# First top-p attention of a four-layer GNN kernel: two row tiles at a time, seven block products in place of eight

## The chip, the cores and the metric

The kernel runs on one core of a Trainium2 chip. The metric is device time in microseconds. Three runs of the kernel before have a median of 3461.52 us, from 3460.03 to 3462.5.

## What is computed

A graph of 3327 nodes with 256 features, `x`, and a dense float32 adjacency `adj` (3327 x 3327) go through four layers, each with a residual and a layernorm, `x = LN(x + layer(x))`. Layer 0 is a mean aggregation with a linear map of `[x, adj @ x / deg]`. Layer 1 is a graph convolution followed by a Mamba scan over the nodes. Layer 2 is a graph attention with a mask. Layer 3, the one that changes, is cut from the reference here:

```python
q = X @ W1.T @ W2.T
k = X @ W3.T
logits = q @ k.T / TAU
probs = jax.nn.softmax(logits, axis=-1)
idx = jnp.argsort(-probs, axis=-1)
sp = jnp.take_along_axis(probs, idx, axis=-1)
cs = jnp.cumsum(sp, axis=-1)
keep_sorted = cs - sp < TOP_P
...
A = probs * mask
return A / jnp.maximum(A.sum(-1, keepdims=True), 1e-12)
...
R = S + jnp.eye(N, dtype=X.dtype)
R = R / R.sum(-1, keepdims=True)
...
for n in range(STEPS):
    A = _top_p_attention(Xa, W1, W2, W3)
    Xf = R @ Xf
    Xa = A @ Xa
    Z = Z + Xf @ U1[n].T + Xa @ U2[n].T
h = X + Z
```

Here `S` is the adjacency, `TOP_P` is 0.9, `STEPS` is 2, and a layernorm of `h` follows. Diffusion (`R @ Xf`) and weighted sum (`A @ Xa`) are each a product of a 3327 x 3327 matrix with a 3327 x 256 matrix, once per step.

## The kernel before

The nodes lie in 26 tiles of 128 rows (`nt = 26`, padded to 3328), and 13 is `nh`. Everything is float32. The name `X` is the layer's input, held in SBUF as 26 tiles of 128 x 256. The adjacency lies in DRAM in transposed blocks (`adjT[tile]`: 128 partitions, 26 blocks of 128 columns), so that a block is at once the stationary operand of a matmul. In the names of the profile, "PE MATMUL acc<-X,at" is such a product: out, then moving and stationary operand. A product over all nodes of one row tile is 26 matmuls of 256 columns into one PSUM bank.

The work is staged in the order of the layers.

- *Layer 0* (L113 to L223). It already works on two row tiles at a time in the seven products of Strassen and Winograd. `halved` (L113) takes the two row tiles as the rows of a 2 x 2 block matrix, whose columns are the first and the second 13 nodes' tiles; the features are split in two halves of 128 (`HD`). It loads five block columns of both rows (`JS`, two DMAs on SP's queue), and VectorE makes three sums or differences of blocks, s2, s3, s4, in `cb`, and the fourth, s1, in place over the block a21. For each of the 13 block columns, seven matmuls of 128 or 129 columns follow. The sums t1 to t4 of the right side are made once. When a pair of tiles is done, VectorE (with one ScalarE copy) puts its four output blocks together from the seven results p1 to p7.
- *Layers 1 and 2.* The change leaves their order as it is. At the end of layer 2, while `X` is finished, the diffusion of tile 0 (`xf0`) is computed, and the keys `kT` and queries for the first attention too. Queries go through DRAM (`qd`).
- *First attention* (`l3p`, a loop from -1 to 25 over row tiles). `scores` (L1116) makes the 3328 logits of a row tile in four groups: two products of query and key into one two-bank PSUM tile `sc`, which has one buffer, and a ScalarE copy into `e`. `diffused` with `aggregated` (L1142, L1157) is a row of R @ X: blocks in loads of five (`J3`), 26 products, and a VectorE operation that adds the node's own part and divides by the degree. `search_short` (L1229) finds the threshold of the nucleus: 26 MAX8 operations on segments of 128 columns, six rounds of ranking the candidates (`ranked`), the exponential of the row on ScalarE, the point at which the running sum crosses (`crossing`), and one VectorE operation that sets the smaller weights of the row to zero and sums the kept ones. `attended` (L1172) is the weighted sum: four transposes of `e` through PE into a bank `tp`, a ScalarE copy into `wt`, four products with `X`, seven times over. `normalizer` gives one over the kept sum. `first` (L1376) ends a row tile: ScalarE scales the weighted sum (`xa`), PE transposes the two results and VectorE copies them to `xt` (L1386), PE multiplies with U1 and U2 of both steps, the sum so far goes to DRAM (`sd`), the products for the second step stay in SBUF as `Y` and `G`, and `key_and_query` (L879) makes key and query of the second attention.
- *Second attention* (`l3q`). It uses that the maps U1 and U2 of step two are already in `Y` and `G`: diffusion multiplies with `Y`, the weighted sum with `G`. Its order of work is written out slot by slot and pinned; its first search (lines L1366 and around) needs the score row of tile 0, and that one needs all keys of the first attention.

What sets the order. Each engine works its own instructions in one order, which is fixed when the kernel is built; engines wait for each other by semaphores. In layer 0 and the first attention a scheduler chooses that order by which instruction is ready and by priority (the score products have a raised one); pools decide how far ahead it can go, since a tile of a pool with two buffers cannot be written again until the one before the last is released. In the second attention, and wherever `keep_in_program_order` (`here`, `in_order`) stands, the order is that of the program. All loads and stores here are issued by SP, in order; one that waits for its data or buffer holds those behind it.

Of the kernel before, what the change touches and what calls it, by code (L numbers as in the profile page):

```python
# [9 lines left out]
F32 = mybir.dt.float32  # L10
BF16 = mybir.dt.bfloat16
# [31 lines left out]
DL = 1  # L43
HD = D // 2
JS = 5
KC = 416
# [3 lines left out]
def gnn_kernel(ctx: ExitStack, tc: tile.TileContext, n: int, a: dict, out: bass.AP):  # L50
# [7 lines left out]
    small = ctx.enter_context(tc.tile_pool(name="small", bufs=4))  # L58

# [53 lines left out]
    def halved(atp, cmb, psum, i, top, low, t):  # L113
# [5 lines left out]
        for j0 in range(0, nh, JS):  # L119
# [4 lines left out]
            cb = cmb.tile([P, 3, JS, P], F32, name="cb")  # L124
            a11, a12, s1, a22 = (at[:, r, h, :m, :] for r in range(2) for h in range(2))
            s2, s3, s4 = (cb[:, k, :m, :] for k in range(3))
            nc.vector.tensor_sub(s3, a11, s1)
            nc.vector.tensor_add(s1, s1, a22)
            nc.vector.tensor_sub(s2, s1, a11)
            nc.vector.tensor_sub(s4, a12, s2)  # L130
# [44 lines left out]
    with tc.tile_pool(name="l1b", bufs=1) as wpool, tc.tile_pool(name="l1at", bufs=2) as l1at:  # L175
# [3 lines left out]
        with tc.tile_pool(name="l0", bufs=1) as pool, tc.tile_pool(name="l0w", bufs=2) as work, \  # L179
# [30 lines left out]
            for i in range(nh):  # L210
                p1, p2, p3, p4, p5, p6, p7 = halved(atp, cmb, psum, i, top, low, ts)
                c = work.tile([P, 2, D + 1], F32, name="c")
                u = work.tile([P, 2, HD + 1], F32, name="u")
                nc.scalar.copy(u[:, 0, :], p1)
                nc.vector.tensor_add(c[:, 0, :HD + 1], p2, u[:, 0, :])
                u2, u3 = u[:, 0, :HD], u[:, 1, :HD]
                nc.vector.tensor_add(u2, p6, u2)
                nc.vector.tensor_add(u3, p7, u2)
                nc.vector.tensor_add(u2, p5[:, :HD], u2)
                nc.vector.tensor_add(c[:, 0, HD + 1:], p3, u2)  # L220
                nc.vector.tensor_sub(c[:, 1, :HD], u3, p4)
                nc.vector.tensor_copy(c[:, 1, HD:HD + 1], p5[:, HD:])
                nc.vector.tensor_add(c[:, 1, HD + 1:], p5[:, :HD], u3)  # L223
# [643 lines left out]
    with tc.tile_pool(name="l3", bufs=1) as pool, tc.tile_pool(name="l3d", bufs=1, space=DRAM) as dram:  # L867
# [10 lines left out]

        def key_and_query(work, ps, p, it, xt):  # L879

            h, j = divmod(it * P, half)
            for k in range(2):
                nc.tensor.matmul(ps, wkq[h][:, k, :], xt[:, k, :], start=(k == 0), stop=(k == 1))
# [205 lines left out]
        sd = dram.tile([nt, P, D], F32, name="sd")  # L1089
# [26 lines left out]
        def scores(work, psum, p, q, e):  # L1116
# [6 lines left out]
            for c0 in range(0, half, KC):  # L1123
# [3 lines left out]
                with tc.high_priority() if not p else nullcontext():  # L1127
                    for h, w in enumerate(ws):
                        k = slice(h * DA, (h + 1) * DA)
                        mm = nc.tensor.matmul(pl[:, h, :w], q[k, :], kT[p][k, c0:c0 + w], start=True, stop=True)  # L1130
                        if p:
                            here(mm)
# [7 lines left out]
                yield  # L1140

# [50 lines left out]
        def segment_tops(cand, z, m=nseg):  # L1192

            for s in range(m):
                nc.vector.max(cand[:, s * 8:(s + 1) * 8], z[:, s * SEG:(s + 1) * SEG])  # L1195
# [4 lines left out]
        def ranked(work, cand, rounds):  # L1200
# [3 lines left out]
            for r in range(rounds):  # L1204
                left = rest if r else cand
                nc.vector.max(top[:, r * 8:(r + 1) * 8], left)
                if r + 1 < rounds:
                    nc.vector.match_replace(rest, top[:, r * 8:(r + 1) * 8], left, NEG)
            return top

        def crossing(work, v, top, base, lim, add=ALU.add, reached=ALU.is_ge):
# [3 lines left out]
            nc.vector.tensor_tensor_scan(cs, ones[:, :k], top, initial=base, op0=ALU.mult, op1=add)  # L1215
            over = work.tile([P, k], F32, name="over", bufs=1)
            nc.vector.scalar_tensor_tensor(over, cs, lim, top, op0=reached, op1=ALU.mult)
            nc.vector.reduce_max(v, over, axis=AX.X)
# [5 lines left out]
        def limit(sm, total):  # L1224
            lim = t1(sm, "lim")
            nc.vector.tensor_scalar_mul(lim, total, TOP_P)
            return lim

        def search_short(work, sm, e, total, v, kept):  # L1229
# [3 lines left out]
            segment_tops(cand, e)  # L1233
            top = ranked(work, cand, RP0)
            neg = t1(sm, "neg")
            nc.vector.tensor_scalar_mul(neg, top[:, 0:1], -1.0)
            nc.scalar.activation(e, e, AF.Exp, bias=neg, accum_out=total)
# [472 lines left out]
```

## Time and profile before

| | |
|---|---|
| median of three runs | 3461.52 us |
| the profiled execution, its own time | 3468.8 us |
| its span, first to last instruction | 3466.9 us |
| mean granted TensorE clock | 0.968 |
| PE busy | 3190.3 us, 92% of the span |
| VectorE busy | 2497.6 us, 72% |
| ScalarE busy | 1742.9 us, 50% |
| loaded from HBM | 291.01 MB |

The span divides as follows. The borders are those of the first and last instruction of a kind in the timeline; busy times in us are from the view by stretches.

| stretch, us | stage | PE busy | DVE busy | ACT busy | clock | DMA share |
|---|---|---|---|---|---|---|
| 0 to 57.9 | layer 0, x and W | 47.1 | 25.7 | 12.7 | 1.00 | 0.61 |
| 57.9 to 324 | layer 0, seven products | 266.0 | 158.7 | 12.4 | 1.00 | 0.46 |
| 324 to 1354 | layer 1 | 854.2 | 878.7 | 673.5 | 0.92 | 0.35 |
| 1354 to 1700 | layer 2 | 335.3 | 245.0 | 53.6 | 0.99 | 0.44 |
| 1700 to 2605.4 | first attention | 888.7 | 419.4 | 318.1 | 1.00 | 0.19 |
| 2605.4 to 3450 | second attention | 798.4 | 768.1 | 671.9 | 0.98 | 0.21 |

How to read it. PE is TensorE's matmuls, PEld its loads of stationary operands, which overlap them; DVE is VectorE, ACT ScalarE, POOL GpSimd, SP the engine that issues the DMAs. The clock is the share of TensorE's full clock that the throttle granted. The DMA share is the mean busy share of the core's 16 DMA engines. Matmuls are pipelined, and several matmuls of one kind can stand in one line of a timeline ("x15"). A bracket at the end of a timeline's line is the idle time ahead of it and what ended it.

### The profile page before, as it was taken

How to read it: one execution, taken by the hardware profiler on the slowest of the kernel's cores; microseconds unless marked ns; L12 is line 12 of the kernel's file. 1: busy time of each engine (PE TensorE's matmuls, PEld its weight loads, DVE VectorE, ACT ScalarE, POOL GpSimd, SP SyncE). 2: the span in 40 equal slices, each digit the busy share in tenths (PEclk: the TensorE clock that was granted, in tenths of full speed). 3: DMA queues.
4: the chain of work that ended last, by engine and by line, in shares of the span. 5: the costliest groups of instructions: out<-in, count | busy, mean ns of one | idle time of the engine just before them, and what ended most of it. 6: DMA issues, size and time to landing. Idle time of an engine off the chain costs nothing. (4 is left out here: it accounts for less than half of the span.)

```text
span 3466.9 us, 45354 instructions
## 1 busy us (share of the span) xinstructions
PE 3190.3 (92%) x16429; PEld 2528.1 (73%) x16429; DVE 2497.6 (72%) x5559; ACT 1742.9 (50%) x2789; POOL 928.5 (27%) x942
## 2 busy tenths in 40 slices
PE   8999888898988766999999999999997999999996
PEld 5998757676666555888777777777775777777775
DVE  4665368999999997777535454545435999999996
ACT  1000556766767774111223333333337888888883
POOL 0000245665655653111100000000001333333333
PEclk9999989999999888999999999999999999999998
DMA  5543334444332222444211212121102122222220
GB/s 168 169 164 126 109 95 125 111 109 115 105 117 82 70 59 108 143 144 149 92 58 55 60 55 60 55 60 55 60 30 77 55 61 71 64 65 70 63 67 16
DMA packets 151760, 304.79 MB, mean 88 GB/s; under 512 B 19454, under 2 KB 65726, under 8 KB 151390
## 3 DMA queue, kind: packets, MB, share of 16 engines
q1 hardware_dynamic: 151518, 301.72, 29.1%
q8 instruction: 133, 2.18, 0.2%
q14 instruction: 109, 0.89, 0.1%
HBM read 291.01 MB, written 10.65 MB: 87 GB/s over the span
## 5 line engine op out<-in xcount | busy, mean ns | idle before, releaser
L329 POOL TENSOR_TENSOR h<-du,row 128x2048 f32<-128x2048 f32 (+1 forms) x110 | 465.6, 4233 | 346.4 <-DVE hc L329 249.8
L329 DVE TENSOR_TENSOR_SCAN h<-dA,carry,h 128x512 f32<-128x512 f32 (+1 forms) x384 | 448.8, 1221 | 18.4 <-ACT dA L336 18.3
L336 ACT ACTIVATE dA<-t,A_log 128x512 f32<-128x512 f32 (+1 forms) x448 | 292.4, 658 | 146.8 <-DVE h L329 145.2
L1183 PE MATMUL acc<-X,wt 128*128 128x256 f32 x1352 | 346.3, 393 | 11.5 <-ACT wt L1181 11.2
L1150 PE MATMUL acc<-F,at 128*128 128x256 f32 x1352 | 353.5, 387 | 1.0 <-ACT q L887 0.6
L1183 PE MATMUL acc<-G,wt 128*128 128x256 f32 x1352 | 336.6, 392 | 6.3 <-ACT wt L1114 5.9
L1183 PEld LDWEIGHTS acc<-X,wt 128*128 128x128 f32 x1352 | 244.4, 191 | 107.1 <-issue 41.3
L1054 PE MATMUL acc<-F,at 128*128 128x257 f32 x1352 | 302.1, 380 | 0.6 <-ACT r L998 0.6
L388 PE MATMUL cb<-F,at 128*128 128x256 f32 x1196 | 295.8, 396 | 6.9 <-ACT hn L408 3.4
L1183 PEld LDWEIGHTS acc<-G,wt 128*128 128x128 f32 x1352 | 250.0, 192 | 66.7 <-ACT wt L1114 36.4
L1195 DVE MAX8 cand<-e 128x8 f32<-128x128 f32 x676 | 142.2, 279 | 213.2 <-ACT e L1136 197.5
L1150 PE MATMUL acc<-X,at 128*128 128x256 f32 x1300 | 295.3, 380 | 0.0
L1150 PEld LDWEIGHTS acc<-F,at 128*128 128x128 f32 x1352 | 237.9, 190 | 75.3 <-issue 50.2
L679 PE MATMUL y<-ident,hc 128*128 128x128 f32 x1664 | 237.1, 297 | 45.6 <-DVE hc L329 45.3
L1054 PEld LDWEIGHTS acc<-F,at 128*128 128x128 f32 x1352 | 252.4, 190 | 36.0 <-issue 1.0
L679 PEld LDWEIGHTS y<-ident,hc 128*128 128x128 f32 x1664 | 211.5, 155 | 86.8 <-DVE hc L329 61.6
L388 PEld LDWEIGHTS cb<-F,at 128*128 128x128 f32 x1196 | 230.3, 199 | 57.4 <-issue 17.4
L1150 PEld LDWEIGHTS acc<-X,at 128*128 128x128 f32 x1300 | 242.3, 190 | 37.7 <-issue 6.6
L329 DVE TENSOR_TENSOR hc<-h,row 128x2048 f32<-128x2048 f32 (+2 forms) x114 | 242.9, 2133 | 11.4 <-PE y L679 4.3
L1181 ACT COPY wt<-tp 128x512 f32<-128x512 f32 (+1 forms) x182 | 93.6, 556 | 302.7 <-PE tp L1179 302.4
L1179 PE MATMUL tp<-ident,e 128*128 128x128 f32 x1352 | 195.3, 275 | 37.7 <-DVE e L1366 32.4
L1179 PEld LDWEIGHTS tp<-ident,e 128*128 128x128 f32 x1352 | 162.3, 142 | 77.9 <-issue 41.1
(383 smaller groups left out, 5761.8 us busy)
## 6 DMA issues: line engine op xcount, KB each, us to landing
at<-in_adjT SPq DMA_DIRECT2D x255, 320.0 KB, 3.0
at<-in_adjT SPq DMA_DIRECT2D x54, 832.0 KB, 4.5
row<-bc SPq DMA_DIRECT2D x80, 512.0 KB, 4.9
at<-in_adjT SPq DMA_DIRECT2D x52, 640.0 KB, 5.4
at<-in_adjT SPq DMA_DIRECT2D x52, 576.0 KB, 4.3
at<-in_adjT SPq DMA_DIRECT2D x26, 512.0 KB, 3.6
row<-bc SPq DMA_DIRECT2D x32, 384.0 KB, 4.8
at<-in_adjT SPq DMA_DIRECT2D x26, 384.0 KB, 4.0
```

The source lines that it names most:

```text
L329: return lambda *x, **k: tc.keep_in_program_order(op(*x, **k))
L336: decays.append(op(*x, **k))
L388: ten.matmul(acc, at[:, j % JC, :], X0[:, j, :], start=(j == 0), stop=(j == nt - 1))
L679: x = ten.matmul(y[:, g * P:(g + 1) * P], h[:, g, i * P:(i + 1) * P], ident, is_transpose=True, start=(first and g == 0), stop=(last and g ...
L1054: nc.tensor.matmul(acc, at[:, j, :], F[:, j0 + j, :], start=(j0 + j == 0), stop=(j0 + j == nt - 1))
L1150: nc.tensor.matmul(acc, at[:, j, :], rhs[:, j0 + j, :], start=(j0 + j == 0), stop=(j0 + j == nt - 1))
L1179: nc.tensor.transpose(pt[:, j, :], e[:, (j0 + j) * P:(j0 + j + 1) * P], ident)
L1181: copy(wt[:, :m, :], pt[:, :m, :])
L1183: nc.tensor.matmul(acc, wt[:, j, :], rhs[:, j0 + j, :], start=(j0 + j == 0), stop=(j0 + j == nt - 1))
L1195: nc.vector.max(cand[:, s * 8:(s + 1) * 8], z[:, s * SEG:(s + 1) * SEG])
```

## The change

*Layer 0.* The block sums get other signs and places: one broadcast operation makes s3 and s1 (each a sum with a21), s2 and s4 follow; the loaded blocks are no longer written over. s2 and s4 of every load are stored to a DRAM array `mixed`, one more DMA on SP's queue per load. The assembly of the outputs follows the signs and no longer uses ScalarE.

*First attention.* The loop goes over 13 pairs of row tiles. Diffusion (`diffused_pair`) and weighted sum (`attended_pair`) of a pair are made of seven products per step, 13 steps, as in layer 0 (`products`, `assembled`). The sums of X (`blocks`, t1 to t4) are made once and lie in the memory of `G`. For diffusion, a part is two steps (`JQ`): three DMAs bring a11, a12, a22 and the stored s2, s4, and one VectorE operation makes s1 and s3 from them. Tile 1, whose pair partner was done in layer 2, is diffused plainly (`diffused_first`). For the weighted sum, a step is four transposes (`turn`: two column blocks of two row tiles), a ScalarE copy into `wt`, and three VectorE operations into `sw` (`mix`). `search_short` is the same work cut into pieces: a yield after every five MAX8, after each ranking round, and the zeroing in two halves. `first` uses the PSUM tiles `tp`, and stores its part of `G` to DRAM (`gd`); two DMAs load `G` at the end of the stage.

*Order.* In this stage every PE and VectorE instruction is held to program order (`Fixed`), all of them recorded at one line. A pair is `stage` with seven diffusion steps, four score groups of one tile and one `first`; seven value steps of the weighted sum; `stage` with the other six diffusion steps, four groups and the other `first`; six value steps. `look` takes the next piece of the search at the head of a queue. Before the loop stand the scores of tile 0, the diffusion of tile 1, the scores of tile 1 and both searches.

In `unresolved`, a small product uses a `tp` tile. The load buffers `l3at` belong to the second attention alone now. The core of the diff:

```diff
@@ -121,13 +123,13 @@
             at = atp.tile([P, 2, 2, JS, P], F32, name="at")
             for r in range(2):
                 nc.sync.dma_start(at[:, r, :, :m, :], a["adjT"][2 * i + r].rearrange("p (h j) r -> p h j r", h=2)[:, :, j0:j0 + m, :])
-            cb = cmb.tile([P, 3, JS, P], F32, name="cb")
-            a11, a12, s1, a22 = (at[:, r, h, :m, :] for r in range(2) for h in range(2))
-            s2, s3, s4 = (cb[:, k, :m, :] for k in range(3))
-            nc.vector.tensor_sub(s3, a11, s1)
-            nc.vector.tensor_add(s1, s1, a22)
-            nc.vector.tensor_sub(s2, s1, a11)
-            nc.vector.tensor_sub(s4, a12, s2)
+            cb = cmb.tile([P, 4, JS, P], F32, name="cb")
+            at = at.rearrange("p r h j k -> p (r h) j k")
+            a11, a12, a21, a22, s3, s1, s2, s4 = (x[:, k, :m, :] for x in (at, cb) for k in range(4))
+            nc.vector.tensor_tensor(cb[:, :2, :m, :], at[:, ::3, :m, :], at[:, 2:3, :m, :].to_broadcast([P, 2, m, P]), op=ALU.add)
+            nc.vector.tensor_add(s2, s1, a11)
+            nc.vector.tensor_add(s4, a12, s2)
+            nc.sync.dma_start(mixed[i][:, :, j0:j0 + m, :], cb[:, 2:, :m, :])
...
+                c = work.tile([P, 2, D + 1], F32, name="c", bufs=1)
+                v, u = c[:, 0, HD + 1:], c[:, 1, HD + 1:]
+                nc.vector.tensor_copy(c[:, 0, :HD + 1], p1)
+                nc.vector.tensor_sub(v, p6, c[:, 0, :HD])
+                nc.vector.tensor_add(c[:, 0, :HD + 1], p2, c[:, 0, :HD + 1])
+                nc.vector.tensor_sub(u, v, p7)
+                nc.vector.tensor_add(v, v, p5[:, :HD])
+                nc.vector.tensor_sub(v, p3, v)
+                nc.vector.tensor_sub(c[:, 1, :HD], u, p4)
...
+        class Fixed:
+
+            def __init__(self, engine):
+                self.engine = engine
+
+            def __getattr__(self, name):
+                op = getattr(self.engine, name)
+                if not fixed:
+                    return op
+                return lambda *x, **k: tc.keep_in_program_order(op(*x, **k))
+
+        tensor, vector = Fixed(nc.tensor), Fixed(nc.vector)
...
+        def products(pa, y, w, b):
+
+            own, mix = pa[:, 0, :], pa[:, 1, :]
+            a11, a12, s1, a22, s2, s3, s4 = w
+            b11, b21, b22, t1, t2, t3, t4 = b
+            for k, (acc, x, v) in enumerate(((own[:, :HD], a11, b11), (own[:, HD:D], a12, b21), (own[:, D:D + HD], s1, t1),
+                                             (mix[:, :HD], s4, b22), (mix[:, HD:D], a22, t4),
+                                             (mix[:, D:D + HD], s2, t2), (mix[:, D + HD:], s3, t3))):
+                tensor.matmul(acc, x, v[:, y, :], start=(y == 0 and k in (0, 3)), stop=(y == nh - 1 and k in (2, 6)))
...
+        def assembled(work, pa):
+
+            p1, p2, p5, p3, p4, p6, p7 = (pa[:, k // 3, k % 3 * HD:(k % 3 + 1) * HD] if k < 6 else pa[:, 1, 3 * HD:] for k in range(7))
+            c = work.tile([P, 2, D], F32, name="c", bufs=1)
+            v, u = c[:, 0, HD:], c[:, 1, HD:]
+            vector.tensor_copy(v, p1)
+            vector.tensor_add(c[:, 0, :HD], p2, v)
+            vector.tensor_sub(v, p6, v)
+            vector.tensor_sub(u, v, p7)
+            vector.tensor_add(v, v, p5)
+            vector.tensor_sub(v, p3, v)
+            vector.tensor_sub(c[:, 1, :HD], u, p4)
+            vector.tensor_add(u, u, p5)
+            return c
...
+        def diffused_pair(quads, psum, i, b, out):
+
+            def part(j0):
+                m = min(JQ, nh - j0)
+                at = quads.tile([P, 5, JQ, P], F32, name="at", bufs=3)
+                rows = [a["adjT"][2 * i + r].rearrange("p (h j) r -> p h j r", h=2)[:, :, j0:j0 + m, :] for r in range(2)]
+                nc.sync.dma_start(at[:, :2, :m, :], rows[0])
+                nc.sync.dma_start(at[:, 2, :m, :], rows[1][:, 1])
+                nc.sync.dma_start(at[:, 3:, :m, :], mixed[i][:, :, j0:j0 + m, :])
+                cb = quads.tile([P, 2, JQ, P], F32, name="cb", bufs=2)
+                vector.tensor_tensor(cb[:, :, :m, :], at[:, 3:4, :m, :].to_broadcast([P, 2, m, P]), at[:, :3:2, :m, :], op=ALU.subtract)
+                a11, a12, a22, s2, s4, s1, s3 = (x[:, k, :m, :] for x, y in ((at, 5), (cb, 2)) for k in range(y))
+                return a11, a12, s1, a22, s2, s3, s4
...
+            pa = psum.tile([P, 2, 512], F32, name="acc")
+            ahead = part(0)
+            yield
+            for j0 in range(0, nh, JQ):
+                w, ahead = ahead, part(j0 + JQ) if j0 + JQ < nh else None
+                for j in range(min(JQ, nh - j0)):
+                    products(pa, j0 + j, [x[:, j, :] for x in w], b)
+                    yield
+            c = assembled(quads, pa)
+            for r in range(2):
+                with_own(c[:, r, :], 2 * i + r, out)
...
+        def attended_pair(quads, psum, es, b):
+
+            pa = psum.tile([P, 2, 512], F32, name="acc")
+            wts, ws = [], []
+
+            def turn(j):
+                pt = psum.tile([P, 4, P], F32, name="tp")
+                for r, e in enumerate(es):
+                    for h in range(2):
+                        tensor.transpose(pt[:, 2 * r + h, :], e[:, (h * nh + j) * P:(h * nh + j + 1) * P], ident)
+                wts.append(quads.tile([P, 4, P], F32, name="wt", bufs=4))
+                nc.scalar.copy(wts[-1], pt)
+
+            def mix():
+                wt = wts.pop(0)
+                sw = quads.tile([P, 4, P], F32, name="sw", bufs=3)
+                vector.tensor_tensor(sw[:, :2, :], wt[:, ::3, :], wt[:, 2:3, :].to_broadcast([P, 2, P]), op=ALU.add)
+                vector.tensor_add(sw[:, 2, :], sw[:, 1, :], wt[:, 0, :])
+                vector.tensor_add(sw[:, 3, :], sw[:, 2, :], wt[:, 1, :])
+                a11, a12, a21, a22, s3, s1, s2, s4 = (x[:, k, :] for x in (wt, sw) for k in range(4))
+                ws.append((a11, a12, s1, a22, s2, s3, s4))
+            for j in range(3):
+                turn(j)
+            for j in range(2):
+                mix()
+            yield None
+            for j in range(nh):
+                if j + 3 < nh:
+                    turn(j + 3)
+                if wts:
+                    mix()
+                products(pa, j, ws.pop(0), b)
+                yield None
+            yield assembled(quads, pa)
...
-            nc.vector.scalar_tensor_tensor(e, e, v, e, op0=ALU.is_ge, op1=ALU.mult, accum_out=kept)
-            yield
+            yield
+            sums = t1(sm, "sums", 2)
+            for h in range(2):
+                part = e[:, h * half:(h + 1) * half]
+                vector.scalar_tensor_tensor(part, part, v, part, op0=ALU.is_ge, op1=ALU.mult, accum_out=sums[:, h:h + 1])
+                yield
+            vector.tensor_add(kept, sums[:, :1], sums[:, 1:])
...
+            pg = psum.tile([P, 4, P], F32, name=tag).rearrange("p (k x) d -> p k (x d)", k=2)
+            for k in range(2):
+                tensor.matmul(pg[:, 0, :], xt[:, 2 + k, :], u2[:, 1, k, :], start=(k == 0), stop=(k == 1))
+            if tag == "pj":
+                nc.scalar.copy(G[:, it, :], pg[:, 0, :])
+            else:
+                g = work.tile([P, D], F32, name="s")
+                nc.scalar.copy(g, pg[:, 0, :])
+                nc.sync.dma_start(gd[it], g)
             key_and_query(work, pg[:, 1, :P], 1, it, xt[:, 2:, :])
...
+                def stage(spread, steps, groups, ends, then=lambda: None):
+                    for k in range(steps):
+                        next(spread, None)
+                        if k % 2:
+                            next(ends, None)
+                        else:
+                            next(groups, None)
+                        if k == 5:
+                            then()
+                        look()
...
+                def attend_to(i):
+                    turned[0] = attended_pair(quads, psum, (es[2 * i], es[2 * i + 1]), b)
+                    finish()
+                    next(turned[0])
...
+                for i in range(nh):
+                    ends = todo or [iter(()), iter(())]
+                    stage(spread, 7, logits(2 * i + 2), ends[0], lambda: attend_to(i))
+                    values = turned[0]
+                    if i + 1 < nh:
+                        queue.append(searches[2 * i + 2])
+                    for _ in range(7):
                         next(values)
-                        if todo is not None:
-                            next(todo)
-                        todo = first(work, psum, i, last_of(values), f, xfs[i])
-                        next(todo)
-                both(todo)
+                        look()
+                    stage(spread, 6, logits(2 * i + 3), ends[1])
+                    for _ in spread:
+                        pass
+                    finish()
+                    if i + 1 < nh:
+                        queue.append(searches[2 * i + 3])
+                    for k in range(6):
+                        if k == 3:
+                            spread = spreading(i + 2)
+                        next(values)
+                        look()
+                        if k % 3 == 2:
+                            look()
+                    c = next(values)
+                    todo = []
+                    for r in range(2):
+                        it = 2 * i + r
+                        f = normalizer(sm, kepts[0][:, it:it + 1], tots[0][:, it:it + 1])
+                        todo.append(first(quads, psum, it, c[:, r, :], f, xfs[it], "tp"))
+                        next(todo[r])
...
+            for x in (slice(0, JH), slice(JH, nt)):
+                nc.sync.dma_start(G[:, x, :], gd[x].rearrange("t p d -> p t d"))
```

## The prediction, made before the result was known

> **What bounds the kernel now.** I read the page's 40 slices first, then the busy time by stretches, then the timelines of PE and DVE inside the stage that changes, then the rows of groups for durations.
>
> ```profile
> PE   8999888898988766999999999999997999999996
> DVE  4665368999999997777535454545435999999996
> PEclk9999989999999888999999999999999999999998
> ```
> The first attention is slices 20 to 30 (1700 to 2605 us): PE full, DVE half full, clock whole. The stretches say the same, with layer 0 on top (columns after the length: busy us and count of PE, PEld, DVE, ACT, POOL; clock; DMA share; GB/s).
>
> ```profile
> 150.00:200.00 50.00, 50.00 (x450) 50.00 (x449) 30.16 (x80) 1.72 (x6) 0.00 (x0) 1.00 0.51 170
> 1900.00:1950.00 50.00, 49.52 (x247) 40.46 (x246) 22.39 (x64) 13.65 (x24) 1.95 (x3) 1.00 0.25 74
> 1950.00:2000.00 50.00, 49.76 (x249) 37.85 (x248) 22.91 (x86) 19.37 (x34) 1.12 (x3) 1.00 0.16 46
> ```
> Two markers of the DVE timeline give the period of one row tile, 1874.17 - 1839.52 = 34.65 us; it is the same for 21 tiles on end.
>
> ```profile
> 1839.52 0.68 DVE L1386 COPY xt<-pj 128x512 f32<-128x512 f32 x1
> 1874.17 0.68 DVE L1386 COPY xt<-pj 128x512 f32<-128x512 f32 x1
> ```
> The PE timeline gives prices. Fifteen matmuls of 256 columns take 3.40 us, the last one's latency 0.38 in it: (3.40 - 0.38)/14 = 0.2157 each (0.2155 over longer runs). A transpose costs 0.11. A score group (four sc matmuls) holds PE 0.9 us and about 0.2 ahead of it: 1.10.
>
> ```profile
> 1815.33 0.97 PE L1130 MATMUL sc<-kT,q 64*128 64x416 f32 x4
> 1816.23 1.56 PE L1183 MATMUL acc<-X,wt 128*128 128x256 f32 x6
> 1821.55 0.71 PE L1179 MATMUL tp<-ident,e 128*128 128x128 f32 x5
> 1822.19 0.97 PE L1130 MATMUL sc<-kT,q 64*128 64x416 f32 x4
> 1828.92 3.40 PE L1150 MATMUL acc<-X,at 128*128 128x256 f32 x15
> ```
> Per tile: 104 products x 0.2155 = 22.4, 26 transposes 2.9, four score groups 4.4, L1384 to L1398 with the key and query 4.3; 34.0, so 0.65 is gaps. PE is the bound and there is next to no wait to remove: only less PE work helps, and PE waits newly made count in full.
>
> [...] Layer 0 runs the same seven products and shows 111 (450 in 50 us); I use the trace. [...] 14.3 us idle, clock 0.50 from 2661, whole at 2676.
>
> ```profile
> 2670.78 1.54 PE L1179 MATMUL tp<-ident,e 128*128 128x128 f32 x6 [14.34 <-DVE e L1366]
> 2661.00:2664.00 3.00, 0.00 (x0) 0.00 (x0) 2.48 (x16) 2.14 (x1) 0.60 (x3) 0.50 0.00 0
> 2673.00:2676.00 3.00, 3.00 (x8) 2.10 (x7) 2.96 (x8) 2.57 (x2) 0.21 (x1) 0.50 0.00 0
> 2676.00:2679.00 3.00, 3.00 (x18) 2.02 (x18) 2.93 (x12) 1.34 (x2) 0.00 (x0) 0.96 0.00 0
> ```
> [...]
>
> **The change, part by part.** A pair is two row tiles; a step is one of its 13 rounds of seven products.
>
> *Products.* Layer 0 makes 169 steps from 59.4 to 323.9: 1.565 us each. A pair costs 13 x 1.565 = 20.35 against 104 x 0.2155 = 22.41 now: 2.06 saved. Not an eighth (2.8), since short matmuls are relatively dearer. Diffusion has 12 pairs (tile 0 belongs to layer 2, tile 1 stays plain), the weighted sum 13: 25 x 2.06 = 51.5 saved. Now the stage is 905.3 = 26 x 34.645 - 11.2 (tile 0's diffusion) + 15.7 of fill and drain. Work after: 889.6 - 51.5 = 838; per pair 65.2.
>
> *DVE work.* Per pair now 2 x (14.6 search + 1.7) = 32.6. Added: 13 mixes of wt into sw (256, 128, 128 columns, each feeding the next: 0.96 us), 12.5; seven cb differences of 512 columns at 0.65, 4.6; two assemblies of eight 128-column operations, 2.0 each; 0.4. Sum about 54 of 65: not a bound in the mean. Cover: PE's own work.
>
> *Fixed order.* It holds DVE and PE to program order, so I laid the queues of one pair side by side with the durations above. Stage 1 is seven diffusion steps, four score groups, one tile's first() (4.4) and 12 transposes: 11.0 + 4.4 + 4.4 + 1.4 = 21.2 us of PE. Then 7 value steps of 2.07, a step and its four transposes; stage 2, six diffusion steps, four groups and a first(), 18.2; 6 value steps, three of them without transposes, 10.9. Together 64.8, near the 65.2 above. Four waits come out.
> - End of stage 2: DVE does the assembly (2.0), two scalings (0.8), half a masking (2.0), then mixes 9 to 12 with 20 MAX8 (5 per 0.98) and one cb between them; mix 12 is done 13.5 after the last diffusion product, when PE has got to its third product at 12.6: 0.75.
> - DVE then still has a MAX group and three ranking rounds (0.9 each), so it is 2.9 late when PE ends the pair. Assembly, normalizer (0.35) and the ACT scaling (0.45) follow, so c is there at 2.9 + 2.0 + 0.35 + 0.45 = 5.7; PE is at its transposes after two steps, a group and two transposes, 4.45: 1.25.
> - Key and query in the same tp bank wait for ACT's copy g (0.37 plus hand-over, as 0.46 in this trace at the last tile; elsewhere other work stood between): 0.45 twice.
> - The second group of the 12 transposes waits for a tp bank that the query copy frees: 0.35.
> Sum 3.25; with one pair less affected, 11 x 3.25 + 1 = 37. Unknown from both sides: 1.0 if DVE is a tenth faster than laid out (only the bank waits stay), 6 if a tenth slower. Not below nothing: each is a new order. I take 3.25.
>
> *Queues.* Behind each waiting DVE instruction stand the MAX8 and ranking of the next tile, and PE's transposes of e wait for those; slack there is only 0.3 us. SP: 65 blocks a pair instead of 52 and one more store per tile. A part's three loads go out when PE leaves the part two before it, and SP's stores in between wait for DVE's s or ACT's g, both due earlier. Landing for 640 KB rows is 5.4 now; slack 4 to 10. Taken at nothing; 2 us a pair if the runs of 1 KB (2.5 KB now) land in 10.
>
> *Fill.* Score groups 0 and 1 stand alone: each waits for ACT to copy the one before (0.85), 2 us instead of 1.1. DVE subtracts the four blocks (7.6), then waits for tile 1's diffusion (1718.6), and does both searches one after the other: e of tile 1 is ready near 1748.7, with 32.7 us of PE work before it. That is 15.9 idle, plus 2.7 at half clock. *Drain.* With no diffusion left, PE waits for the last search (3.6), for the mixes (1.5), and does three first() without cover: 60.4 against 44.1 of work, 16.3, plus 1.5 of clock. Both 36.4, bounds 24 and 46.
>
> *G through DRAM.* The second half of G (1.7 MB) and the first at loads stand behind the last g store on SP, so the second attention's first products come about 10 us late. PE waits 14.3 us there anyway for tile 0's search (the line above), and that search's scores are now issued without products between, 2 us earlier. -2; +6 if SP takes longer.
>
> *Layer 0.* 640 KB of stores per five steps: DMA share 0.50 goes to about 0.75. The next load is ahead of the store in SP's order; combos keep their element count; the ACT copy goes. Nothing, bound +10.
>
> Sum: 838 + 37 + 36.4 = 911.4, +6; -2 and 0: +4, less 1 for waits that fall together: **+3**. The profiled execution would be 3468.8 + 3 (span 3466.9 + 3); the median of the runs shown, 3461.5, goes to **3464**.
>
> **Rivals.**
> - *Fed queues (0.24).* DVE never falls behind; waits 1.0 a pair: 838 + 12 + 30 = 880, -25 and -2: 3435. For it: DVE is half idle now. Against it: the order is rigid and its slack is tenths.
> - *DVE sets the pace (0.18).* Slower. Place: mix 12 and the half-maskings ahead of the 12 transposes. From the point where DVE ends a pair over 3 us late, each further us passes to PE. A tenth on 54 us of DVE or one late cb load makes it 6 a pair: 12 x 3 more, 3500.
> - *Layer 0's stores delay its loads (0.08).* PE is full there, so 1 us per load group shows: 39 groups, some 10 to 30 us, 3485.
> - That the seven products do not save: layer 0 shows that they do; in none of these.
>
> **Numbers.** Likeliest 0.50, own range 3452 to 3476. The range 3430 to 3496 leaves out the ends of the first two rivals, some 0.18. A measurement of this kernel can tell 0.2% (7 us) from no change: faster than 3454.6 is the first rival and a tenth of the likeliest, 0.28; slower than 3468.4 is the two slow ones and a third of it, 0.42; the rest 0.30.
>
> **What would show it.** Products: PE's 128-column matmuls at 0.111 to 0.112 each. Period of a pair 68 to 69 (69.3 now), PE idle before acc<-sw and tp<-c with DVE named, DVE 80% full. First transposes of e near 1750 and half clock after it. Second attention's start within 5 us of where it was. Wrong: a pair at 66 (first rival) or over 70 (second), or layer 0 ending after 330.

## The result, and the profile after

The changed kernel takes 3493.84 us (median of four runs, 3488.59 to 3494.34), the kernel before beside it 3462.01 us (3460.03 to 3464.72): ratio 1.0088, 95% interval 1.007 to 1.0105. It is 32 us slower; the forecast was 3464, within 3430 to 3496. The profiled execution after took 3488.6 us (span 3486.7), the one before 3468.8: only 19.8 apart, since the first lies 5 us below its kernel's median and the second 7 above its own. What the medians show beyond the 19.8 is taken up at the end of the experiments.

The page's slices for PE, VectorE and the clock, kernel after:

```profile
PE   8999888888987777999899999999978999999996
DVE  4665368999999997777577777787755999999996
PEclk9999999999999988999899999999998999999998
```
VectorE is now 7 where it was 4 to 5, and PE has a hole (7, 8) at the end of the first attention. By stretches (columns as before: busy us and count of PE, PEld, DVE, ACT, POOL; clock; DMA share; GB/s) these are layer 0, one pair in the middle of the stage, its first 56 us and its last 70:

```profile
150.00:200.00 50.00, 50.00 (x450) 50.00 (x449) 29.57 (x74) 1.19 (x4) 0.00 (x0) 1.00 0.72 249
1874.42:1942.96 68.54, 65.34 (x499) 57.03 (x498) 51.94 (x178) 24.41 (x39) 0.20 (x2) 1.00 0.25 75
1696.30:1752.70 56.40, 41.20 (x180) 28.05 (x181) 38.54 (x111) 17.68 (x20) 19.52 (x20) 0.76 0.32 97
2554.37:2624.12 69.75, 50.47 (x330) 44.09 (x330) 30.27 (x99) 15.87 (x36) 0.20 (x2) 0.93 0.13 43
```
Layer 0 still has PE full, with the DMA share at 0.72 instead of 0.51. The period of a pair is read at the same copy as before, here at every second one on VectorE's timeline:

```profile
1874.42 0.68 DVE L891 COPY xt<-tp 128x512 f32<-128x512 f32 x1
...
1942.96 0.68 DVE L891 COPY xt<-tp 128x512 f32<-128x512 f32 x1
```
A pair takes 68.54 us against 2 x 34.65 = 69.3: the products save 4.1 (the forecast's twice 2.06), and 3.3 of it are lost again, nearly all in waits. The view of PE's waits in this pair (us in total, times, longest):

```profile
PE tp L891 <- ACT c L1532: 1.4, 1, 1.4
PE tp L891 <- ACT s L1558: 0.9, 2, 0.5
PE acc L891 <- DVE sw L891: 0.6, 2, 0.5
PE tp L891 <- ACT q L903: 0.2, 1, 0.2
```
That is 3.1 us with PE idle. VectorE's longest waits in the same pair:

```profile
DVE s L891 <- PE tp L891: 8.1, 2, 4.1
DVE xt L891 <- PE tp L891: 2.4, 1, 2.4
DVE sw L891 <- ACT wt L1253: 1.7, 1, 1.7
```
So each of the two engines waits for the other within one pair. VectorE is not overloaded (52 of 68.5 us).

Three lengths divide every kernel below: up to the first score product of tile 0 (layers 0 to 2), from there to the start of the last product of key and query (the first attention), and the rest. "Pair" is the period of a pair of row tiles.

| kernel | layers 0 to 2 | first attention | rest | pair | first transposes of e after the stage's start |
|---|---|---|---|---|---|
| before | 1699.2 | 904.8 | 862.8 | 69.29 | 38.3 |
| after | 1696.3 | 926.5 | 863.9 | 68.54 | 56.4 |

The first attention is 21.7 us longer: 11 periods of a pair give 11 x 0.75 = 8 back, so its two ends cost some 30 more than before.

### The profile page after: what moved, and what is told of

Same layout as the page of the kernel before. It is cut to its first block, busy times and chain, and to the rows that moved or that the text cites. A ratio compares the mean times of both kernels' runs of the same rounds, so it can differ in the third digit from the quotient of the medians.

```text
span 3486.7 us, 50559 instructions
## 1 busy us (share of the span) xinstructions
PE 3154.8 (90%) x18379; PEld 2568.2 (74%) x18379; DVE 2759.1 (79%) x6406; ACT 1742.3 (50%) x2763; POOL 939.7 (27%) x942
## 5 line engine op out<-in xcount | busy, mean ns | idle before, releaser
L1319 PEld LDWEIGHTS acc<-G,wt 128*128 128x128 f32 x1352 | 249.1, 192 | 65.2 <-ACT wt L1130 35.6
L891 PEld LDWEIGHTS acc<-X,at 128*128 128x128 f32 x988 | 143.5, 194 | 49.0 <-issue 44.8
L891 PE MATMUL acc<-X,at 128*128 128x128 f32 (+1 forms) x988 | 177.9, 292 | 0.0
L891 PE MATMUL acc<-G,sw 128*128 128x128 f32 x1014 | 169.7, 276 | 6.0 <-DVE sw L891 6.0
L138 PE MATMUL acc<-t,cb 128*128 128x128 f32 (+1 forms) x1014 | 168.4, 275 | 0.0
L1253 ACT COPY wt<-tp 128x512 f32<-128x512 f32 x169 | 98.7, 588 | 131.8 <-PE tp L891 117.0
L891 PEld LDWEIGHTS acc<-G,sw 128*128 128x128 f32 x1014 | 140.3, 192 | 8.2 <-DVE sw L891 8.1
```

The costliest lines, as they stand in the source:

```text
L138: mm = nc.tensor.matmul(acc, w[:, j, :], x, start=(y == 0 and k % 3 == 0 and k < 6), stop=(y == nh - 1 and k in (2, 6)))
L891: return lambda *x, **k: tc.keep_in_program_order(op(*x, **k))
L1319: nc.tensor.matmul(acc, wt[:, j, :], rhs[:, j0 + j, :], start=(j0 + j == 0), stop=(j0 + j == nt - 1))
```

## The experiments

The length of the first attention repeats within 1.5 us (904.8, 905.3, 905.0 and 903.8 in four kernels that have the old one), while the length of layers 0 to 2 lies anywhere in some 10 us (1692.9 to 1702.5) in the fourteen profiled executions, one for each kernel. So causes in the stage are read from the stage.

### No fixed order

```diff
-                fixed = True
+                fixed = False
```


> The changed kernel without the fixed order in the first attention: the scheduler places PE and VectorE instructions. Theory (the waits of a pair and the idle time of the fill are made by the order, VectorE waiting for tile 1's diffusion ahead of tile 0's search): the fill shortens by some 8 us and the pair loses a part of its 3.3 us of waits, 10 to 30 us faster than the changed kernel. Rival (the order is better than what the scheduler makes, and the waits come from the data): the same time or slower, up to 40 us.

Measured: 3453.24 us, ratio to before 0.9966 (0.9955 to 0.9976). Stage 889.6; pair 66.35 to 66.5 in seven of eleven periods, the others up to 67.6; first transposes of e after 44.8. Of PE's waits in the pair one is left, and VectorE stands less ahead of `s` (3.7 us instead of 8.1) and waits for logits as they come instead (waits in one pair, 1928.46 to 1994.81):

```profile
PE tp L1537 <- ACT c L1532: 0.7, 1, 0.7
```
```profile
DVE cand L1370 <- ACT e L1151: 7.1, 5, 2.9
DVE s L1547 <- PE tp L1545: 3.7, 2, 2.2
```
With the same instructions in another order the stage is 37 us shorter, and the kernel is faster than both. The fixed order is the cause of the stage's slowdown; the rival falls.

### Which engine's order

Only PE held, or only VectorE held:

```diff
-        tensor, vector = Fixed(nc.tensor), Fixed(nc.vector)
+        tensor, vector = Fixed(nc.tensor), nc.vector
```


> The changed kernel with only PE held to program order, VectorE left to the scheduler. Without any fixed order the stage took 889.6 us (first scores to last key and query) against 926.5 with it, and a pair 66.35 against 68.5. Theory (it is VectorE's order that costs: it stands idle 4.0 and 4.2 us ahead of the additions s and 2.4 ahead of xt, with search work behind them in the queue, and is then late for mix 12 and for c): a pair near 66.4 to 67, stage 885 to 900. Rival (PE's order costs): a pair at 68 or more, stage 915 to 927.

```diff
-        tensor, vector = Fixed(nc.tensor), Fixed(nc.vector)
+        tensor, vector = nc.tensor, Fixed(nc.vector)
```


> The changed kernel with only VectorE held to program order, PE left to the scheduler. Theory (VectorE's order costs): a pair near 68, stage 915 to 927, total as the changed kernel. Rival (PE's order costs): a pair near 66.4, stage 885 to 900.

PE held: stage 906.7, a pair about 67.5, 3472.20 us (1.0025, 1.0012 to 1.0038). VectorE held: stage 900.0, a pair 66.28, 3462.76 us (0.9996, 0.9987 to 1.0005). My theory, that VectorE's order alone costs, fell: freeing PE helps more, and freeing either takes away the wait for `sw` (0.5 us or less in nine pairs). Most of the loss needs both orders: of the 37 us, 17 stay with PE alone held and 10 with VectorE alone. With PE free the additions `s` still stand in VectorE's queue (61.0 us of waiting for PE in nine pairs), but PE puts other work where VectorE is late.

### More of the search ahead of the additions

VectorE's timeline in the changed kernel, second half of a pair:

```profile
1912.42 0.41 DVE L891 TENSOR_TENSOR cb<-at 128x256 f32<-128x256 f32 x1
1916.99 0.42 DVE L891 TENSOR_TENSOR s<-tp,X 128x256 f32<-128x256 f32 x1 [4.15 <-PE tp L891]
1917.33 0.37 DVE L891 MAX8 top<-rest 128x8 f32<-128x208 f32 x1
...
1921.21 0.29 DVE L891 COPY c<-acc 128x128 f32<-128x128 f32 x1 [0.31 <-PE acc L891]
...
1924.34 1.94 DVE L891 SCALAR_TENSOR_TENSOR e<-e,v 128x1664 f32<-128x1664 f32 x1
```
The ranking round at 1917.33 had its data by 1912.5 (the round before ends with the replacement in `rest`, 0.36 us from 1912.14) and stood behind `s` for 4 us; so the second half of the masking comes after the assembly, at 1924.34, ahead of the mixes. The edit takes two pieces of the search per step:

```diff
                             then()
                         look()
+                        look()
```


> The changed kernel, order fixed, but two pieces of the search per step of a stage instead of one, so that VectorE has them ahead of the additions s at which it stands idle 4 us. Theory: in the second half of a pair the search is done before the assembly, the last mix comes 1.9 us earlier and the waits for sw (0.64 per pair) and c (1.44) go: a pair 66.4 to 66.9 instead of 68.5, 18 to 25 us faster than the changed kernel. Rival (VectorE is late because of its load, not because of where its work stands): a pair stays within 0.5 us of 68.5.

Measured: pair 66.58, stage 900.6, 3467.43 us, ratio to before 1.0007 (0.9998 to 1.0016), 26 us below the changed kernel's median. The same place, with the search ahead of `s` and masking done before the assembly:

```profile
1910.24 1.95 DVE L891 SCALAR_TENSOR_TENSOR e<-e,v 128x1664 f32<-128x1664 f32 x1
...
1913.95 0.42 DVE L891 TENSOR_TENSOR s<-tp,X 128x256 f32<-128x256 f32 x1 [1.42 <-PE tp L891]
1914.30 1.94 DVE L891 SCALAR_TENSOR_TENSOR e<-e,v 128x1664 f32<-128x1664 f32 x1
...
1918.17 0.29 DVE L891 COPY c<-acc 128x128 f32<-128x128 f32 x1 [1.73 <-PE acc L891]
```
PE's waits for `sw` are gone and that for `c` is 0.7. Where the work stands was the cause, not how much it is: one line, order still fixed, gives nearly the whole of what the free order gives per pair.

### Key and query a step apart from the product that shares their bank

```diff
+            if tag == "tp":
+                yield
             key_and_query(work, pg[:, 1, :P], 1, it, xt[:, 2:, :])
...
-                        if k % 2:
+                        if k in (1, 3, 4, 5):
                             next(ends, None)
-                        else:
+                        if k % 2 == 0:
                             next(groups, None)
```


> The changed kernel with the key and query product one diffusion step after the product that shares its bank. Theory (each wait of a pair counts in full): both waits of 0.46 us per row tile go, a pair takes 67.6 us instead of 68.5, 10 to 12 us faster than the changed kernel. Rival (VectorE's chain sets the pair, the time comes back at the next wait on it): a pair stays at 68.3 or more and the wait for the scaled weighted sum (1.44 us) or for the last mix (0.48) grows by what was saved.

Both waits of 0.46 are gone, but the pair is 68.66 and the stage 927.2 (3492.09 us; 1.0081, 1.0062 to 1.01): the rival's number. PE's timeline of this kernel:

```profile
1933.91 0.49 PE L891 MATMUL acc<-G,sw 128*128 128x128 f32 x2 [1.26 <-DVE sw L891]
1934.56 0.49 PE L891 MATMUL acc<-X,sw 128*128 128x128 f32 x2 [0.17 <-DVE sw L891]
1941.58 0.44 PE L891 MATMUL tp<-ident,c 128*128 128x128 f32 x2 [1.42 <-ACT c L1532]
```
and the changed kernel's at the same place:

```profile
1934.30 0.49 PE L891 MATMUL acc<-G,sw 128*128 128x128 f32 x2 [0.47 <-DVE sw L891]
1934.95 0.49 PE L891 MATMUL acc<-X,sw 128*128 128x128 f32 x2 [0.16 <-DVE sw L891]
1941.99 0.44 PE L891 MATMUL tp<-ident,c 128*128 128x128 f32 x2 [1.44 <-ACT c L1532]
```
0.8 of the 0.9 saved comes back as a longer wait for the mix. That this is VectorE's chain, as the rival has it, is not shown, for the edit did more than remove waits. The product that shares the bank (`tp<-U,xt` x4) is what moved: in the second half of a pair it now stands ahead of the last diffusion step, and VectorE's assembly needs that step. PE's and VectorE's timelines of this kernel:

```profile
1917.09 1.03 PE L891 MATMUL tp<-U,xt 128*128 128x256 f32 x4
...
1920.39 0.39 PE L891 MATMUL acc<-G,cb 128*128 128x128 f32 x2
```
```profile
1915.73 0.42 DVE L891 TENSOR_TENSOR s<-tp,X 128x256 f32<-128x256 f32 x1 [4.15 <-PE tp L891]
...
1920.81 0.29 DVE L891 COPY c<-acc 128x128 f32<-128x128 f32 x1 [1.18 <-PE acc L891]
```
and PE's in the changed kernel:

```profile
1920.78 0.39 PE L891 MATMUL acc<-G,cb 128*128 128x128 f32 x2
1921.00 1.03 PE L891 MATMUL tp<-U,xt 128*128 128x256 f32 x4
```
So the assembly starts 5.1 us after the second `s` instead of 4.2 (1916.99 to 1921.21 in the changed kernel, shown above). The pair's first half, from the copy `xt` at 1874.42 to the next, is 0.74 us shorter (35.01 against 35.75); no assembly follows the moved product there. The second half is 0.86 longer (33.65 against 32.79). So the wait in the first half did count, and what it gained was lost by what now stands ahead of VectorE's work in the second. Whether the wait there is slack was not tested.

### The weighted sum without the seven products

```diff
+            def plain(j, wt):
+                for r in range(2):
+                    for h in range(2):
+                        tensor.matmul(pa[:, r, :D], wt[:, 2 * r + h, :], X[:, h * nh + j, :], start=(j == 0 and h == 0), stop=(j == nh - 1 and h == 1))
...
-            for j in range(2):
-                mix()
...
-                if wts:
-                    mix()
-                products(pa, j, ws.pop(0), b)
+                plain(j, wts.pop(0))
```


> The changed kernel, order fixed, with the weighted sum of a pair as four plain products of 256 columns per step instead of seven of 128: no mixes, no assembly of it. PE gets 13 x (4 x 0.2155 - 7 x 0.1113) = 1.08 us more per pair, VectorE 14.5 us less. Theory (the waits for sw and c, 2.1 us per pair, come from VectorE): they go, a pair near 67.4, some 10 to 15 us faster than the changed kernel, though its PE work is larger. Rival (PE alone sets the pair): a pair near 69.6, 10 to 15 us slower.

The 1.08 in this text is wrong: a float32 product stands as two records in the trace (eight for the four products of a step; in the changed kernel 2366 for the 1183 of the weighted sums), so the plain sum adds twice that. Measured, a step with its transposes takes 2.16 us instead of 2.00: 13 x 0.16 = 2.1 us more PE work a pair (PE busy 66.73 instead of 65.34). Even so a pair takes 67.84, 0.7 less, stage 909.5, 3475.44 us (1.0028, 1.0018 to 1.0038). Only these waits are left on PE in a pair:

```profile
PE tp L891 <- ACT s L1559: 0.9, 2, 0.5
PE tp L891 <- ACT q L903: 0.2, 1, 0.2
```
In this fixed order the seven products of the weighted sum cost more, by what they ask of VectorE, than they save PE.

### The ends of the stage

First the prologue: scores of tile 1 directly after those of tile 0, the end of tile 1's diffusion after both searches.

```diff
+                for _ in logits(1):
+                    look()
+                alone = diffused_first(quads, psum, 1, xfs)
+                for _ in range(4):
+                    next(alone)
+                    look()
+                finish()
+                spread = spreading(1)
...
+                for _ in alone:
+                    pass
```


> The changed kernel with another prologue: scores of tile 1 right after those of tile 0, and VectorE's last operation of tile 1's diffusion after both searches instead of in the middle of the first one. Theory (in the fill VectorE stands 9.2 us behind PE's diffusion of tile 1, and that is the critical chain): first transposes of e some 10 us earlier (near 1742 instead of 1752.7), 8 to 12 us faster than the changed kernel. Rival (PE's own work and the half clock bound the fill): within 3 us of the changed kernel.

Neither theory nor rival held: first transposes after 61.8 us, stage 931.3 (3495.05 us; 1.0087, 1.007 to 1.0104). The 9.2 us wait did go, and another took its place (VectorE's timeline of this kernel):

```profile
1743.63 0.69 DVE L891 TENSOR_TENSOR cb<-at 128x512 f32<-128x512 f32 x1 [13.48 <-DMA at<-mixed]
1744.24 5.12 DVE L891 MAX8 cand<-e 128x8 f32<-128x128 f32 x26
```
I had moved tile 1's diffusion behind the second scores. The three load buffers `at` come free only as PE uses them (in the changed kernel's first attention SP waits 331.6 us for PE ahead of the loads into them, in 71 waits), so the first part of pair 1 landed late, and its difference `cb` stood ahead of the second search.

Then the diffusion of a pair moved into its own pair, on top of the two search pieces and on top of the free order:

```diff
-                            spread = spreading(i + 2)
+                            spread = spreading(i + 1)
```
(with `diffused_first` as the first pair's diffusion and both searches ahead of the loop)

> The changed kernel, order fixed, with two search pieces per step (m1_looks: stage 900.6 us, pair 66.58) and the diffusion of a pair moved from the pair before into its own, so that pair 12's lies at the end of the stage where PE stands idle, and not in the fill; both searches of the fill then follow each other on VectorE. Theory (fill and drain cost because PE has no work that is ready there, about 32 us idle to the first xt and 19 after the last score row): the 20.35 us of PE work leave the fill, which VectorE bounds, and lie in the drain's gaps; stage 886 to 895. Rival (the fill is bound by PE's own work and half clock, the drain by its chain of first): stage 898 to 906.

> The changed kernel without the fixed order (stage 889.6 us) and with the diffusion of a pair moved into its own pair, as in the kernel before it. Theory: as there, 5 to 12 us less, stage 878 to 885, the fastest so far, near 3445. Rival: stage within 3 us of 889.6 or above, since the scheduler had already pulled other work into the gaps.

Fixed order: stage 899.6 against 900.6, 3461.44 us (0.9999, 0.9991 to 1.0008): the rival's number, but its account holds only in part. The drain did take work: from the sixth-last copy `xt` to the end PE idles 12.7 us instead of 20.5, and this stretch takes 9.5 us longer for some 20 us more of work. The fill, here up to the first `xt`, lost as much work and became only 10.5 us shorter, for PE idles 25.5 us there instead of 16.7: 18.0 of them (11.7 before) ahead of score groups, which wait until ScalarE has copied the group before out of the only `sc` tile, and 5.8 for the masked row `e`. In the drain the last two `first` keep their gaps, since they come after all products (PE's timeline, changed kernel):

```profile
2606.63 0.44 PE L891 MATMUL tp<-ident,c 128*128 128x128 f32 x2 [3.11 <-ACT c L1532]
...
2615.11 0.71 PE L891 MATMUL tp<-xt,wkq 128*128 128x128 f32 x4 [1.85 <-ACT s L1558]
...
2622.77 0.71 PE L891 MATMUL tp<-xt,wkq 128*128 128x128 f32 x4 [1.63 <-ACT s L1558]
```
Free order: stage 884.0, 5.6 less, as the theory had it, and the shortest of all; 3449.99 us, 0.9961 of before (0.9946 to 0.9977). By the total it cannot be told from the free order alone (0.9966). No run gave `sc` a second buffer, though in the changed kernel 11.5 of the 15.2 us that PE idles before the first transposes are waits for these copies.

### Layer 0 alone

The kernel before with layer 0's part: first whole, then without this store, then without the DRAM array too.

```diff
+            nc.sync.dma_start(mixed[i][:, :, j0:j0 + m, :], cb[:, 2:, :m, :])
```


> The kernel before with layer 0's part of the change alone: other signs, s2 and s4 stored, nobody reads them. Theory (the loss lies in the first attention, at its two ends): within 3 us of before, layer 0 ending at 323 to 324 in the profile as before. Rival (the stores delay loads or something outside the first attention costs the part of the 32 us that the two profiles do not show, 12 us): 8 to 15 us slower than before.

> The kernel before with layer 0's part of the change, but without the store of s2 and s4. With the store it was 1.0019 of before (1.0007 to 1.003), while its first attention took 905.3 us against 904.8. If the stores cost it (they are the only new transfers): ratio back at 1.000, within 0.0007. If the placing of buffers or the new block sums cost it: ratio stays near 1.002. If it was scatter of layers 1 and 2: either.

> The kernel before with layer 0's new block sums and assembly alone: no store, and not even the DRAM array for it. Without the store but with the array the ratio to before stayed at 1.0017 (1.001 to 1.0025), though the first attention took 905.0 us as before. If it is the array (the other DRAM buffers lie elsewhere, and layers 1 and 2 load from them): ratio 1.000, within 0.0007. If it is the new instructions of layer 0 (another state of clock or queues handed to layers 1 and 2): ratio stays near 1.0017.

Ratios 1.0019 (1.0007 to 1.003), 1.0017 (1.001 to 1.0025), 1.0022 (1.0012 to 1.0032), some 6 to 8 us. Neither store nor array is the cause; what is left is the new block sums and assembly, with their buffers. Where they cost it stays open: in the profiles layer 1's first product starts at 325.9 to 326.7 with the edit and 326.9 without, and the first attention keeps its length, so it would lie in layers 1 and 2, whose instructions are the same and whose time scatters by as much. It was not narrowed further. Every kernel above that starts from the changed one carries it too. By the medians, 32 - 21.7 (stage) - 1.1 (rest) leaves 9 for layers 0 to 2, and these 6 to 8 would be most of it; the two profiles, in which layers 0 to 2 are 2.9 shorter after, do not show it.

## Why the prediction came out as it did

The range held the time, and that is luck in part: the likeliest case, 3464, is 30 us short and its own range ends at 3476. What reaches up to 3496 are cases that did not happen, above all VectorE setting the pace (3500). None of the listed signs of being wrong looked at the two ends of the stage, where the time went. Step by step:

| step | forecast | measured |
|---|---|---|
| PE work of a pair | 65.2 us | 65.34 busy |
| waits of a pair | 3.25: mix 0.75, c 1.25, keys 0.9, bank 0.35 | 3.1: 0.6, 1.4, 0.9, 0.2 |
| period of a pair | 68 to 69 | 68.54 |
| VectorE per pair | 54 us | 51.9 |
| fill and drain | 36.4 (24 to 46) | 51 |
| from the last product of key and query to the next attention's first transposes | -2 | +0.6 (67.35; 66.73 before) |
| layer 0 | nothing, bound +10 | ends at 323.7 (324.2 before); alone +6 to +8, place open |

*Products, pair, waits* were right, each in its place. (What the prediction counts as products, 104 of 256 columns per tile, are records, two to a product; its sums hold, since it takes the times of records.) The two waits of key and query, 0.46 us each, are for ScalarE's copy `s` of other columns of the same PSUM bank; why PE waits there for other columns, no run shows. For f32 additions the trace of the kernel before has 0.82 us at 640 columns (L127 to L130), 0.425 at 256 (L1400) and 0.28 to 0.29 at 128 (L217 to L223). What the forecast puts on the new ones was my estimate, and they keep to these times: in this trace the broadcast of the mix, 256 columns, takes 0.41 to 0.43, and its additions of 128 take 0.29.

*Fill and drain* is the term that failed: stage 926.5 less 838 of work and 12 x 3.1 of waits leaves 51, 15 over the forecast and above its upper bound. Some 5 of the 15 lie in the fill, ahead of the first transposes of e: 56.4 us, where the forecast makes 32.7 of work, 15.9 idle and 2.7 of half clock, 51.3 in all. The idle time was right (15.2), the half clock was not. It came three times, ahead of the first transposes and not after them as I had expected (a line's first numbers after the length: PE busy and PEld busy; the last three: clock, DMA share, GB/s):

```profile
1700.03:1710.27 10.24, 8.34 (x21) 4.20 (x18) 10.14 (x23) 2.62 (x4) 10.24 (x6) 0.50 0.49 169
1723.92:1734.16 10.24, 5.28 (x16) 2.85 (x17) 9.44 (x28) 6.01 (x7) 0.00 (x0) 0.50 0.13 41
1740.99:1747.82 6.83, 6.00 (x23) 4.60 (x24) 3.98 (x14) 2.53 (x4) 0.00 (x0) 0.50 0.08 27
```
PE is busy for 19.6 us of these. Eight records of tile 1's diffusion take 3.78 us in the first of them (from 1706.37), twenty take 4.48 at full clock (from 1712.70), so a record takes about twice as long and half the clock costs about 9.8 (an estimate from these lines). The forecast's 2.7 was my estimate. The half clock that the prediction shows lies in and after 14.34 us with PE idle; ahead of the first stretch here no idle time is longer than 2.35 us (PE busy for 1.87 us of the 5.03 from 1695.00, short score groups between waits), and the clock was 0.50 all the same. How much idle time brings it, no run shows. VectorE passes the delay on: it stands idle until PE has done the score groups and the diffusion of tile 1, and goes on 23.6 us after the stage's start, not 19.4 (1718.6 by the forecast, with the start at 1699.2). Later it stands behind one more `cb`. Its timeline there:

```profile
1706.72 3.95 DVE L891 MAX8 cand<-e 128x8 f32<-128x128 f32 x20
1719.89 0.48 DVE L891 SCALAR_TENSOR_TENSOR F<-acc,rdeg,F 128x256 f32<-128x256 f32 x1 [9.21 <-PE acc L891]
...
1748.69 0.69 DVE L891 TENSOR_TENSOR cb<-at 128x512 f32<-128x512 f32 x1 [3.19 <-PE acc L891]
1749.30 1.95 DVE L891 SCALAR_TENSOR_TENSOR e<-e,v 128x1664 f32<-128x1664 f32 x1
```
Some 8 more lie in the drain: 69.75 us where I had 61.9. Of that, 19.3 are idle instead of 16.3, and PE is busy for 50.5 us where I had 44.1 of work and 1.5 of clock; two stretches of half clock, with PE busy for 8.6 us in them, explain some 4 of the difference (the sixteen records of `tp<-U,xt` take 5.92 and 5.41 us there and 3.69 at full clock). The bound was made for durations at full clock with one wait late at a time.

*The hand-over* gained nothing: G's loads came in time (the second goes out at 2625.35, behind the last store of `gd` at 2622.75, and lands 6.9 us later, and G is first read at 2691.9), and the scores of tile 0 without products between them ran at half clock (four groups at 1.75 us from 2626.09 on, 0.97 at full clock).

*Fed queues*, the fast rival, gave its number for a pair almost exactly (waits 1.0), but only once the order was free. What I held against it, a rigid order with little slack, is what the runs show. *VectorE sets the pace* had a wrong mechanism: no tenth of load was missing, and a pair never reached 70. What the forecast did not see is that two of the waits it listed, for the mix and for `c`, came from one place, VectorE standing ahead of `s` with work behind it: one line that moved search work ahead of that wait took away the first and half of the second.

## What to carry to other kernels

When two engines with long queues are both held to a written order, lay their waits out side by side. What paid here was to move ready work ahead of the instruction at which the other engine stands idle; to move a product in order to save a wait gained nothing where it then stood ahead of something that the other engine needed. A saving per period is only worth counting after the two ends of the stage, at the clock that was granted there (0.76 in the fill and 0.93 in the drain here), have been priced with it. And before an order is written out by hand, measure the scheduler's: here it made the stage 37 us shorter.
